# Attention and mixture layer in one kernel: two buffers for reloaded rows, a fuller start on TensorE, and a later last product

## The chip, the cores and the metric

The kernel runs on one core of a Trainium2 chip. The metric is the time of one execution on the device, in microseconds (us); lower is better. A core has five engines that work side by side, each through its own list of instructions in order: TensorE (PE, matrix products, with PEld for its weight loads), VectorE (DVE), ScalarE (ACT), GpSimd (POOL) and SyncE (SP). Transfers (DMA) are issued by SP, ACT and POOL. An instruction that waits holds up all that stands behind it in its engine's list. This is also so for a transfer that waits: it holds up the transfers behind it in the same issuing list.

## The reference

The input is x, 1024 rows of 512 numbers in float32, and the kernel computes

```
xn = layernorm(x)
q, k, v = xn @ w_q, xn @ w_k, xn @ w_v      # 32 query heads, 8 key/value heads, 128 wide
attn = softmax(causal(q k^T / sqrt(128))) v   # 4 query heads share one key/value head
x = x + layernorm(attn @ w_o)
h = layernorm(x)
w = weights of 8 experts from the 8 largest of 15 router probabilities of h
y = h @ base_W^T + base_b + 2 * sum over experts of w_e * (h A_e^T) B_e^T
out = x + layernorm(y)
```

## The kernel before, in words

The 1024 rows are eight tiles of 128. At the start all rows of x are loaded and normalized in place (`input_norms`, L238), and each tile is turned by four TensorE transposes and one copy by ACT into `xnT` (`input_turn`, L262). Values come from `project_v`, keys from `project_k`, and queries for two row tiles at once from `project_q` (two banks, each holding two of the four heads of a key/value head).

The attention is then worked off in 64 blocks. A block is one key/value head g and one row tile t, with its four query heads (`blocks`, L88). The list runs over heads 0 to 5 with all eight tiles each; the last sixteen blocks, 48 to 63, alternate between heads 6 and 7 in pairs of tiles: (6,0) (6,1) (7,0) (7,1) (6,6) (6,7) (7,6) (7,7) (6,4) (6,5) (7,4) (7,5) (6,2) (6,3) (7,2) (7,3). The width of a block's tiles is 128 (t+1), so a block can be told in the profile by its widths.

Each block has four parts n (`scores`, L358): 32 rows of all four heads. A part is a product q k^T on TensorE (`s`), a mask addition and a maximum on VectorE (L378, L380), an exponential on ACT (L385), a reciprocal on POOL (L387), and, one part later, the scaling by ACT (L391) and a 32 by 32 transpose on VectorE into the tile `T` (L394). After the fourth part `to_keys` (L403) issues 16 transfers that put T into the layout `K`; they are issued by SP, and for the very last block by SP and ACT in turn (L399). Two blocks later `weighted_values` multiplies K with v (`po`). T and K have one buffer for even and one for odd tiles.

Work between the parts of a block is laid down in the loop of L698: the list `then` is cut by its estimated cost into four shares, one behind each part (`run_share`). It holds projections for coming blocks, the product with v of block i-2, and the output projection of earlier blocks, which for heads 0 to 6 is done for a pair of row tiles (`project_o_pair`, seven products in place of eight), and for head 7 by `project_o`.

When head 7 is done for a row tile, its attention output is complete, and the second half of the layer begins for this tile: `reload_x` (L533) brings the row of x back at i = k+2 for block k, issued by SP at the beginning of block i, ahead of the K transfers of block i-1; `project_o` at k+3 is followed by `ffn_norms`, which adds x at L519; `ffn_router` comes at k+5, `ffn_out` at k+6 or k+7, and `ffn_store` (L593), again issued by SP at the beginning of a block, at k+7 or k+8. `ffn_out` consists of two products with base_W, a transpose of the expert rows (`ptw`, copied by ACT into `hwT`), two more products, and a last product with hwT, after which VectorE computes y, its norm and the sum into `acc` (L586 to L588). The last four of the eight row tiles are completed behind the loop, from L727 on.

The order of instructions on VectorE, ACT and POOL that is not fixed by the program (marked by `keep`) is set by a scheduler when the kernel is built; transfers and TensorE's instructions stay in the program's order.

Of the kernel before, what the change touches and what calls it, by code (L numbers as in the profile page):

```python
# [22 lines left out]
def kernel(  # L23
# [74 lines left out]
    def transpose(*args):  # L98
        keep(nc.tensor.transpose(*args))

    def load(dst, src, by=nc.sync):
        keep(by.dma_start(dst, src))  # L102
# [86 lines left out]

    def prepare_mask():  # L190

        mask = const.tile([P, P], F32, tag="mask", name="mask")
        make_causal_mask(nc, mask, mask_val=MASKED)
        for h in range(R):
            keep(nc.vector.tensor_copy(smask[ts(h, SQ), :], mask[ts(h, SQ), ts(h, SQ)]))
# [29 lines left out]
    def bank(name):  # L225
        return ps_m.tile([P, 512], F32, tag="pm", name=name)
# [35 lines left out]
    def input_turn(t):  # L262
        transposed(xnT[t // TPB][:, :, ts(t % TPB, P)], x_in[:, t, :], f"x{t}")
# [18 lines left out]
    def project_v(gv, t):  # L282
        def finish(pm):
            v = vs[gv, t] = act.tile([P, GV * D], F32, tag="v", name=f"v_{gv}_{t}", bufs=NT + 2)
            nc.scalar.copy(v, pm)

        def term(c):
            return xnT[t // TPB][:, c, ts(t % TPB, P)], weights["v", gv, c]

        return chained(  # L290
            lambda: bank(f"pv_{gv}_{t}")[:, : GV * D],
            [lambda c=c: term(c) for c in range(KC)],
            finish,
            GV * D,
        )

    def project_k(g, qb):
        def finish(pm):
            kT = kTs[g, qb] = act.tile([P, QB], F32, tag="kT", name=f"kT_{g}_{qb}", bufs=2 * NQB)
            nc.scalar.copy(kT, pm)  # L300

        def term(c):
            return weights["k", g][:, c, :], xnT[qb][:, c, :]

        return chained(
            lambda: bank(f"pk_{g}_{qb}"), [lambda c=c: term(c) for c in range(KC)], finish
        )

    def project_q(g, u):

        pm = {}

        def get(j):
            if j % 2 == 0:
                pm[0] = bank(f"pq_{g}_{u}_{j}")
            return pm[0][:, ts(j % 2, PQ)]

        def finish(j):
            if j == 0:
                qTs[g, u] = act.tile([P, PQ // SQ, R, SQ], F32, tag="qT", name=f"qT_{g}_{u}")  # L320
            if j % 2:
                nc.scalar.mul(  # L322
                    qTs[g, u][:, :, j - 1 : j + 1, :].rearrange("p s h q -> p h s q"),
                    pm[0].rearrange("p (h s q) -> p h s q", h=2, q=SQ),
                    scale,
                )

        def term(j, c):
            w = weights["q", j // 2]
            assert w[0] == g  # L330
            rhs = xnT[u * PQ // QB][:, c, ts(u % (QB // PQ), PQ)]
            return w[1][:, c, ts(j % 2, D)], rhs

        work = []
        for j in range(R):
            terms = [lambda j=j, c=c: term(j, c) for c in range(KC)]
            if j == 0:
                ends = lambda pm: finish(0)
            else:
                ends = lambda pm, j=j: finish(j)  # L340
            work += chained(lambda j=j: get(j), terms, ends, PQ)
        return work
# [15 lines left out]
    def scores(g, t, j):  # L358

        n = t * P + (j + 1) * SQ  # L360
        full = (t + 1) * P
        name = f"{g}_{t}_{j}"

        if t < TPB and j % 2:
            s = score_tile.pop(0)[:, QB:]
        else:
            s = ps_s.tile([P, S], F32, tag="s", name=f"s_{name}")
            score_tile[0] = s
        for c0 in range(0, n, QB):
            w = min(QB, n - c0)  # L370
            matmul(
                s[:, c0 : c0 + w],
                qTs[g, t // 2][:, (t % 2) * NSUB + j, :, :].rearrange("p h q -> p (h q)"),
                kTs[g, c0 // QB][:, :w],
                start=True,
                stop=True,
            )
        nc.vector.tensor_tensor(s[:, n - SQ : n], s[:, n - SQ : n], smask, ALU.add)  # L378
        nmax = small.tile([P, 1], F32, tag="nmax", name=f"nmax_{name}")
        nc.vector.tensor_reduce(nmax, s[:, :n], AX.X, ALU.max, negate=True)  # L380
        p = act.tile([P, S], F32, tag="p", name=f"p_{name}", bufs=3)
        if n < full:
            nc.gpsimd.memset(p[:, n:full], 0.0)  # L383
        total = small.tile([P, 1], F32, tag="total", name=f"total_{name}")
        nc.scalar.activation(p[:, :n], s[:, :n], AF.Exp, bias=nmax, accum_out=total)  # L385
        rec = small.tile([P, 1], F32, tag="rec", name=f"rec_{name}")
        nc.gpsimd.tensor_tensor(rec, total, neg_one, ALU.pow)  # L387
        finish_scores()

        def finish():  # L390
            keep(nc.scalar.mul(p[:, :n], p[:, :n], rec))  # L391
            if j == 0:
                turned[g, t] = turn_view(turn_tile("T", g, t), t)
            nc.vector.transpose(  # L394
                turned[g, t][:, :, j, :, :].rearrange("p b k q -> p k b q"),
                p[:, :full].rearrange("p (k b q) -> p k b q", b=R, q=SQ),
            )
            if j == NSUB - 1:
                to_keys(g, t, by=two if (g, t) == blocks[-1] else two[:1])  # L399

        score_tile["finish"] = finish

    def to_keys(g, t, by=(nc.sync,)):  # L403

        src = turned.pop((g, t))
        dst = keyed[g, t] = turn_view(turn_tile("K", g, t), t)
        for h in range(R):
            for b in range(NSUB):
                load(dst[ts(b, SQ), h, :, :, :], src[ts(h, SQ), b, :, :, :], by[b % len(by)])

    attnT = {}

# [97 lines left out]
    state = {}  # L510

    def reload_x(t):
        xt = state["x", t] = ffn.tile([P, H], F32, tag="x", name=f"xr_{t}", bufs=1)
        load(xt, x[ts(t, P), :])

    def ffn_norms(t):
# [77 lines left out]
        load(out[ts(t, P), :], acc[t])  # L594


    def projections(i):


        g, t = blocks[i]  # L600
        q, other = [], []
        m = i // 2 + 1
        if i % 2 and m < len(pairs):
            q = project_q(*pairs[m])
        if i < N2:
            if t == 2:
                other += project_k(g, 1)
            if t == 6:
                other += project_k(g + 1, 0)
            if g == 0 and t < 2:  # L610
                other += [(P * KC, lambda n=n: input_turn(n)) for n in range(TPB + 2 * t, TPB + 2 * t + 2)]
                other += project_v(0, 2 + t)
            elif g % GV == 0 and (g or t >= TPB):
                other += project_v(g // GV, t)
        else:
            n = i - N2
            for k, what in ((0, (G - 1, 0)), (2, (G - 2, 1)), (3, (G - 1, 1))):
                if n == k:
                    other += project_k(*what)
            for t in {0: (0,), 1: (1,), 2: (2, 3), 3: (4, 5), 4: (6, 7)}.get(n, ()):  # L620
                other += project_v(g // GV, t)
        return q, other
# [25 lines left out]
    def run(pieces):  # L648
        for _, f in pieces:
            f()  # L650
# [23 lines left out]
    input_norms(range(TPB))  # L674
    prepare_mask()
    input_norms(range(TPB, NT))
    for t in range(TPB):
        input_turn(t)
        if t < 2:
            run(project_v(0, t))  # L680
    run(project_k(0, 0))
    run(project_q(0, 0))
    load_o(0, nc.sync)
    combine_o(0)

# [12 lines left out]
    for i in range(N):  # L698
        loads(i)
        for t in complete(i, 2):  # L700
            reload_x(t)
        for t in complete(i, 7, 8):
            ffn_store(t)
        q, other = projections(i)
        pv = attend(i - 2) if i >= 2 else []
        o, o_pair, ends, begins = [], [], [], []
        for t in complete(i, 3):
            o = project_o(*blocks[i - 3])
        if i % 2 == 0 and i >= 4 and blocks[i - 4][0] < G - 1:
            o_pair = project_o_pair(*pairs[i // 2 - 2])  # L710
        for t in complete(i, 6, 7):
            ends = sum(ffn_out(t), [])
        for t in complete(i, 5):
            begins = ffn_router(t)

        then = begins[:1] + q + ends + o + weave(o_pair, begins[1:] + other + pv)
        for n in range(NSUB):
            scores(*blocks[i], n)
            run_share(then, n, NSUB)
        if i == NT:  # L720
            prepare_ffn()

        if i >= NT and blocks[i - 2][1] == 0 and blocks[i - 2][0] < G - 1:
            combine_o(blocks[i - 2][0])
# [63 lines left out]
```

## Time and profile before

| | us |
|---|---|
| median of three runs | 1124.17 |
| lowest, highest | 1122.99, 1276.79 |
| the profiled execution | 1121.25 |
| its span in the profile | 1119.5 |
| TensorE busy | 1073.8 |
| VectorE busy | 639.3 |
| ACT busy | 464.3 |
| POOL busy | 230.2 |

The profile is of one execution. Its lines name the engine, the line of the program, the operation and the tiles (result <- operands), then the count, busy time, and in brackets how long the engine was idle before and what ended that. A row of the stretches gives the stretch, its length, then for PE, PEld, DVE, ACT and POOL the busy time and the number of instructions, the clock granted to TensorE (1.00 is full), the busy share of the transfer engines, and GB/s. A row of waits gives who waited for whom: the total, the number of times and the longest. A row of the timeline gives the start, the length from the first to the last instruction of the group, and the group. SPq is SP's list of transfers, as far as it is issued.

A float32 product shows as two matmul instructions, a transpose as one.

### The profile page before, as it was taken

The numbers are of one execution on the slowest core, as the hardware profiler recorded it, in microseconds if no ns is written. First come the engines' busy times: TensorE is split into PE (matmuls) and PEld (weight loads), VectorE is DVE, ScalarE is ACT, GpSimd is POOL, SyncE is SP. The second block draws the span as 40 slices with busy tenths as digits, with TensorE's granted clock in tenths as the row PEclk, the third lists the DMA queues.
The fourth block names the chain that finished last, engine by engine and source line by source line (L and its number), as shares of the span: only waits on it lengthen the run. The fifth ranks groups of instructions, "written<-read, shape, count | busy, mean of one in ns | idle before, by whom it ended". The sixth has DMA issues, their size and how long they took to land.

```text
span 1119.5 us, 12689 instructions
## 1 busy us (share of the span) xinstructions
PE 1073.8 (96%) x3816; PEld 702.7 (63%) x3816; DVE 639.3 (57%) x1285; ACT 464.3 (41%) x985; POOL 230.2 (21%) x524
## 2 busy tenths in 40 slices
PE   6999999999999999999999999999999699999796
PEld 4676666667676666666676666666776356466353
DVE  4466545664566545665465546665346556766665
ACT  2544434444354434444344434543335343353310
POOL 5311113111321113111221113111131111211200
PEclk9999999999999999999999999999999899999998
DMA  6145332555135332555135332556241743552420
GB/s 208 34 109 131 76 86 56 146 127 109 34 97 136 79 85 57 125 139 116 36 88 137 87 85 57 133 137 155 62 121 50 173 116 73 146 137 53 99 75 29
DMA packets 79380, 111.82 MB, mean 100 GB/s; under 512 B 18176, under 2 KB 50960, under 8 KB 79312
## 3 DMA queue, kind: packets, MB, share of 16 engines
q1 hardware_dynamic: 53552, 82.38, 31.8%
q10 hardware_dynamic: 25424, 27.79, 8.1%
q0 software_dynamic: 336, 0.83, 0.2%
q8 instruction: 31, 0.51, 0.2%
q14 instruction: 37, 0.30, 0.1%
HBM read 33.34 MB, written 2.10 MB: 32 GB/s over the span
## 4 chain that ended last, share of the span: by engine, by line
PE 84%; DVE 5%; ACT 4%; SPq 3%; POOL 1%; issue 1%; DMA 1%; ACTq 0%; POOLq 0%; DVEq 0%
PE po L96 20%; PE s L96 18%; PE pq L96 17%; PE pv L96 5%; PE pk L96 5%; PE pa L96 4%; PE pe L96 4%; SPq L102 3%; PE pc L96 2%; PE pb L96 2%; PE pd L96 2%; PE pf L96 2%; ACT p L385 2%; PE pO L96 2%; DVE nmax L380 1%; DVE T L394 1%
## 5 line engine op out<-in xcount | busy, mean ns | idle before, releaser
L385 ACT ACTIVATE p<-s,nmax 128x32 f32<-128x32 f32 (+31 forms) x256 | 179.6, 702 | 440.3 <-DVE nmax L380 401.8
L394 DVE STREAM_TRANSPOSE T<-p 128x128 f32<-128x128 f32 (+7 forms) x256 | 198.5, 776 | 218.8 <-ACT p L391 193.1
L96 PE MATMUL po<-K,v 128*128 128x512 f32 x576 | 279.2, 599 | 15.9 <-DMA K<-T 14.8
L96 PE MATMUL s<-kT,qT 128*128 128x512 f32 (+15 forms) x768 | 274.2, 466 | 6.0 <-ACT p L385 5.3
L387 POOL TENSOR_TENSOR rec<-total,neg_one 128x1 f32<-128x1 f32 x256 | 143.7, 562 | 637.2 <-ACT p L385 636.9
L96 PE MATMUL pq<-xnT,wq 128*128 128x256 f32 x1024 | 234.9, 379 | 0.0
L96 PEld LDWEIGHTS s<-kT,qT 128*128 128x128 f32 x768 | 145.5, 191 | 134.1 <-issue 110.3
L96 PEld LDWEIGHTS pq<-xnT,wq 128*128 128x128 f32 x1024 | 193.1, 190 | 38.7 <-issue 15.6
L391 ACT ACTIVATE p<-p,rec 128x32 f32<-128x32 f32 (+31 forms) x256 | 185.6, 725 | 2.9 <-POOL rec L387 2.7
L380 DVE TENSOR_REDUCE nmax<-s 128x1 f32<-128x32 f32 (+31 forms) x256 | 180.7, 706 | 7.4
L96 PEld LDWEIGHTS po<-K,v 128*128 128x128 f32 x576 | 107.9, 191 | 91.7 <-issue 75.5
L378 DVE TENSOR_TENSOR s<-s,smask 128x32 f32<-128x32 f32 x256 | 49.1, 192 | 148.8 <-PE s L96 148.3
L96 PE MATMUL pv<-wv,xnT 128*128 128x256 f32 x256 | 69.8, 388 | 1.3 <-ACT xnT L236 1.3
L322 ACT ACTIVATE qT<-pq 128x512 f32<-128x512 f32 x64 | 38.0, 593 | 66.4 <-PE pq L96 66.3
L96 PE MATMUL pk<-xnT,wk 128*128 128x512 f32 x128 | 64.6, 594 | 0.7 <-ACT xnT L236 0.7
L383 POOL MEMSET p<- 128x96 f32 (+2 forms) x192 | 29.0, 152 | 166.5 <-DVE T L394 160.5
L96 PE MATMUL pa<-wo,attnT 128*128 128x256 f32 x224 | 61.9, 385 | 0.0
L419 ACT COPY attnT<-po 128x512 f32<-128x512 f32 x64 | 37.2, 581 | 54.1 <-PE po L96 47.4
L96 PEld LDWEIGHTS pv<-wv,xnT 128*128 128x128 f32 x256 | 48.9, 194 | 11.9 <-issue 2.7
L96 PEld LDWEIGHTS pa<-wo,attnT 128*128 128x128 f32 x224 | 41.0, 190 | 17.8 <-issue 13.9
L385 ACT ACTIVATION_READ_ACCUMULATOR p<-s,nmax 128x1 f32 x256 | 49.7, 194 | 0.0
L96 PE MATMUL pe<-wo,sums 128*128 128x256 f32 x112 | 32.2, 379 | 0.0
(101 smaller groups left out, 731.5 us busy)
## 6 DMA issues: line engine op xcount, KB each, us to landing
K<-T SPq DMA_DIRECT2D x128, 128.0 KB, 2.4
K<-T SPq DMA_DIRECT2D x128, 112.0 KB, 2.3
wq<-in_w_q_dram ACTq DMA_DIRECT2D x27, 512.0 KB, 4.8
K<-T SPq DMA_DIRECT2D x128, 96.0 KB, 2.2
K<-T SPq DMA_DIRECT2D x128, 80.0 KB, 2.1
K<-T SPq DMA_DIRECT2D x120, 64.0 KB, 2.0
wo<-in_w_o_dram ACTq DMA_DIRECT2D x28, 256.0 KB, 3.8
K<-T SPq DMA_DIRECT2D x128, 48.0 KB, 1.9
```

The source lines that it names most:

```text
L96: keep(nc.tensor.matmul(*args, **kw))
L102: keep(by.dma_start(dst, src))
L322: nc.scalar.mul(qTs[g, u][:, :, j - 1 : j + 1, :].rearrange("p s h q -> p h s q"), pm[0].rearrange("p (h s q) -> p h s q", h=2, q=SQ), scale,)
L378: nc.vector.tensor_tensor(s[:, n - SQ : n], s[:, n - SQ : n], smask, ALU.add)
L380: nc.vector.tensor_reduce(nmax, s[:, :n], AX.X, ALU.max, negate=True)
L383: nc.gpsimd.memset(p[:, n:full], 0.0)
L385: nc.scalar.activation(p[:, :n], s[:, :n], AF.Exp, bias=nmax, accum_out=total)
L387: nc.gpsimd.tensor_tensor(rec, total, neg_one, ALU.pow)
L391: keep(nc.scalar.mul(p[:, :n], p[:, :n], rec))
L394: nc.vector.transpose(turned[g, t][:, :, j, :, :].rearrange("p b k q -> p k b q"), p[:, :full].rearrange("p (k b q) -> p k b q", b=R, q=SQ),)
L419: nc.scalar.copy(o, po)
```

## The change

It has six parts.

- `reload_x` takes two buffers (the pool's default) in place of one. The room for it comes from `prepare_mask`, whose mask is now a slice of one of the three softmax tiles `p`.
- At the start, 20 transposes of the identity matrix into a bank that nobody reads stand ahead of the first turn of x.
- The first projections are reordered: tile 2 is turned ahead of the values of tile 1, the queries of the first two heads stand ahead of the keys, and tiles 4 and 5 are turned ahead of the first scores. Tiles 6 and 7 follow in blocks 0 and 1.
- The queries of the second pair of row tiles, all in block 1 before, are divided between blocks 0 and 1.
- The last product of `ffn_out` inside the loop stands four pieces of the other work further on.
- The K transfers of the last block are issued by SP (11) and POOL (5) in place of SP (8) and ACT (8).

```diff
-        mask = const.tile([P, P], F32, tag="mask", name="mask")
+        mask = act.tile([P, S], F32, tag="p", name="mask", bufs=3)[:, :P]
...
-                to_keys(g, t, by=two if (g, t) == blocks[-1] else two[:1])
+                three = (nc.sync, nc.sync, nc.gpsimd)
+                to_keys(g, t, by=three if (g, t) == blocks[-1] else three[:1])
...
-                load(dst[ts(b, SQ), h, :, :, :], src[ts(h, SQ), b, :, :, :], by[b % len(by)])
+                load(dst[ts(b, SQ), h], src[ts(h, SQ), b], by[(h * NSUB + b) % len(by)])
...
-        xt = state["x", t] = ffn.tile([P, H], F32, tag="x", name=f"xr_{t}", bufs=1)
+        xt = state["x", t] = ffn.tile([P, H], F32, tag="x", name=f"xr_{t}")
         load(xt, x[ts(t, P), :])
...
+    later = {}
+
     def projections(i):
...
         m = i // 2 + 1
-        if i % 2 and m < len(pairs):
+        if i == 0:
+            later["q"] = project_q(*pairs[m])
+            q = later["q"][: 2 * KC]
+        elif i == 1:
+            q = later["q"][2 * KC :]
+        elif i % 2 and m < len(pairs):
             q = project_q(*pairs[m])
...
             if g == 0 and t < 2:
-                other += [(P * KC, lambda n=n: input_turn(n)) for n in range(TPB + 2 * t, TPB + 2 * t + 2)]
+                other += [(P * KC, lambda n=TPB + 2 + t: input_turn(n))]
                 other += project_v(0, 2 + t)
...
     input_norms(range(TPB))
     prepare_mask()
     input_norms(range(TPB, NT))
-    for t in range(TPB):
+
+    idle = bank("idle")
+    for n in range(20):
+        transpose(idle[:, ts(n % KC, P)], ident, ident)
+    input_turn(0)
+    run(project_v(0, 0))
+    for t in range(1, 3):
         input_turn(t)
-        if t < 2:
-            run(project_v(0, t))
-    run(project_k(0, 0))
-    run(project_q(0, 0))
+    run(project_v(0, 1))
+    input_turn(3)
+    first_q = project_q(0, 0)
+    run(first_q[: 2 * KC] + project_k(0, 0) + first_q[2 * KC :])
+    for t in range(TPB, TPB + 2):
+        input_turn(t)
     load_o(0, nc.sync)
     combine_o(0)
...
-        then = begins[:1] + q + ends + o + weave(o_pair, begins[1:] + other + pv)
+        rest = o + weave(o_pair, begins[1:] + other + pv)
+        then = begins[:1] + q + ends[:-1] + rest[:4] + ends[-1:] + rest[4:]
```

## The prediction

> **What bounds the kernel now.** I read the page's share of engines, then TensorE's busy time in stretches. A block is one KV head and one row tile; I number the 64 blocks in their order, so "p52" is the softmax of block 52, "T52" its transposed copy, "K52" the 16 transfers that bring T52 into the layout for the product with v.
>
> ```profile
> PE 1073.8 (96%) x3816; PEld 702.7 (63%) x3816; DVE 639.3 (57%) x1285; ACT 464.3 (41%) x985; POOL 230.2 (21%) x524
> ```
> ```profile
> 60.00:460.00 400.00, 397.99 (x1444) 267.77 (x1443) 229.61 (x433) 178.85 (x375) 82.70 (x191) 1.00 0.40 96
> 460.00:860.00 400.00, 399.41 (x1452) 270.37 (x1451) 218.49 (x403) 175.12 (x369) 80.39 (x183) 1.00 0.42 102
> 860.00:960.00 100.00, 87.65 (x277) 50.26 (x276) 61.90 (x119) 38.60 (x69) 15.35 (x37) 0.95 0.46 109
> 960.00:1060.00 100.00, 93.49 (x304) 53.74 (x303) 65.74 (x159) 39.10 (x90) 21.55 (x49) 0.98 0.46 115
> ```
> The first number after the length is TensorE's busy time: 2.6 us of 800 are idle from 60 to 860, so only TensorE's work counts there and the change leaves it alone. The idle time is at the start, in 860 to 1060 (12.35 + 6.51 us, with the clock down to 0.95), and at the end. The waits of TensorE from 860 on, and SP's queue in the same stretch, say why:
>
> ```profile
> PE po L96 <- DMA K<-T: 14.0, 3, 9.3
> PE pf L96 <- ACT hwT L581: 3.2, 3, 2.1
> ```
> ```profile
> SPq L102 <- DVE acc L519: 30.9, 2, 19.6
> ```
> Reloads of x (xr) stand in SP's queue ahead of K transfers. With one buffer, a reload waits until the previous row has been added at L519. The timeline shows the largest case:
>
> ```profile
> 868.14 0.65 DVE L519 TENSOR_TENSOR acc<-acc,xr 128x512 f32<-128x512 f32 x1
> 868.82 0.33 SPq L102 DMA_DIRECT2D xr<-in_x_dram  x1
> 869.26 20.21 SPq L102 DMA_DIRECT2D K<-T  x32
> ...
> 879.67 0.55 DVE L223 TENSOR_SCALAR h<-acc,mv_h,rstd_h 128x512 f32<-128x512 f32 x1 [0.66 <-POOL rstd_h L222]
> 881.27 2.04 PE L96 MATMUL po<-K,v 128*128 128x512 f32 x2 [9.29 <-DMA K<-T]
> ```
> T52 was finished at 853.5 (its last transposes start at 852.42 and take 1.11), but K52 could leave only at 869.26. TensorE stood 9.29 us and was then slow.
>
> [...] eight matmuls of pv took 3.58 us at 8.43 and 1.99 at 13.12; two of po took 2.04 at 881.27 where 0.86 is usual. [...] Here a K transfer costs SP some 0.59 us. [...]
>
> **The change, part by part** (positions are those of the unchanged trace).
>
> Start. The ACT table load ends at 7.68, so the first xnT copy stays at 7.79 whatever the transposes on the identity do. If they warm the array, pv saves 3.58 - 1.99 = 1.6 us; if not, nothing. Either way the next wait is another: rows 4 and 5 are now turned before the first scores.
>
> ```profile
> 23.94 1.34 POOL L454 TENSOR_TENSOR wot<-wo,wot 128x512 f32<-128x512 f32 x1
> 25.24 1.17 POOL L250 TENSOR_TENSOR rstd_x<-ve_x,neg_half 128x1 f32<-128x1 f32 x2
> ```
> ```profile
> 25.83 0.55 DVE L254 TENSOR_SCALAR K_x<-K_x,mv_x,rstd_x 128x512 f32<-128x512 f32 x1 [0.67 <-POOL rstd_x L250]
> ```
> Row 5 is normalized at 26.38, behind the wo subtractions on Pool, which wait for wo until 19.5; the built order of Pool keeps that. Queries before keys fill TensorE to about 24.0 when warm (25.6 cold), then it waits; first scores at 26.9 instead of 28.01: 1.1 us. Two turns (0.43 us each) are then behind it, and half of the next queries stands between the first scores, whose waits on exp were 0.95 and 0.43. Bounds: 0 (these waits stay) and 3.3 us; I take **1.5**.
>
> Reloads, first case. With two buffers the reload of block 51 passes at about 848, K52 leaves at 853.5 and lands 16 x 0.6 + 2.4 us later, near 866; po52 starts at 871.98 without waiting. What is late next is VectorE: from 872 to 880.22 it does the norms of two rows, then a transpose (1.11), mask and maximum (1.3), exp (1.0), so scores of block 55 start at 883.9 where TensorE could at 881 and where they started at 892.40: 8.5 gained. The 2.9 us stand may cool the array; up to 1.2 us are lost. From there I follow both engines to block 56 (906 against 914.14) and find no further wait. Bounds: 4.4 (what VectorE itself gains) and 9.3 + 2.4 of slow clock; I take **7.4**.
>
> Reloads of blocks 55 and 59: no TensorE wait hung on the former. The latter frees K60 (T60 is ready near 1019, K60 left at 1033.66) and K61, which now leaves when T61 is ready, 1038.2, and lands near 1050.6. The waits of 0.92 and 3.79 us before po60 and po61 go, and with the second some 2 us of slow clock (four matmuls in 3.68 us, usual 1.72). But see below.
>
> Last FFN product further on. TensorE waited 2.09 and 0.66 us for hwT; other products now fill this. Bounds 0.5 and 2.9; I take **2.3**. Its price is that y, its norm and the addition to acc (L586 to L588, 3.8 us before: 1039.51 to 1043.27) are later on VectorE, and the store of that row stands in SP's queue ahead of the next block's K transfers. For blocks 50, 51 and 54 the built order puts the addition ahead of the last transpose that K needs: nothing lost. For block 55 it puts it after T62's: K62 no longer waits for VectorE in its own name, but stands behind out55.
>
> ```profile
> 1054.68 0.53 SPq L102 DMA_DIRECT2D out_dram<-acc  x1
> 1055.32 13.69 SPq L102 DMA_DIRECT2D K<-T  x18
> ```
> ```profile
> 1067.04 1.10 PE L96 MATMUL po<-K,v 128*128 128x512 f32 x2 [0.97 <-ACT p L391]
> ```
> Before, K62 left at 1055.32 and set po62 at 1067.04 (the wait is named p, but is K62: 16 x 0.59 + 2.2 after 1055.32 is 1067). In the new order I place VectorE's instructions with the durations above: T62 ends at 52.7 (1052.7), then statistics 0.69, logits 0.17, aggregate 0.18, mask 0.18, three small ones, maximum 0.62, y 0.55, addition 0.69: acc55 at 56.2, K62 from 56.9, landing at 1068.5, 1.5 later than now. TensorE, without the waits of po60 and po61, is there at 1059.2 and stands 9.3 us; as at 881, 2.4 us of slow clock follow. So the waits taken away return at one place: **-3.9** (bounds +6.7 if K62 were not late, -8).
>
> Final K transfers: ACT's eight issues (1067.82 to 1073.44) go; its next work, attnT, needed po62 at 1073.3 anyway. SP issues 11 and Pool 5, done by about 1075, needed at 1084; the cover is 9 us, and Pool has no work until y's rstd. [...] The mask's tile in a softmax buffer costs one memset behind copies that end at 12.9. Both **0**.
>
> Sum: 1.5 + 7.4 + 2.3 - 3.9 = 7.3. The profiled execution took 1121.25 us, so 1114; the median of the runs is 2.9 above it, so 1117. I say **1116**.
>
> **Rivals.** (B) The store does not hold K62: it leaves at 52.7, lands at 1064.9; TensorE still stands 5 us and cools. 3.6 us better: 1112. For it: acc55's operations are short. (C) All waits go and none returns: 3.3 + 9.3 + 2.9 + 0.92 + 3.79 + 1.96, about 22: 1101. Against it: VectorE's full stretch at 872. (D) The time of K52 comes back on VectorE (4.4 only), the start gives nothing: 1121. (E) Slower: the same store. Every us by which acc55 is later than 1056.2 delays K62, and TensorE, by one. Gains outside the end are 11.2, so the change loses when K62 lands over 8.8 us after 1067, acc55 being then at about 1064; at 1069 it would give 1129. Against it: nothing on VectorE that long stands there.
>
> **Chances.** Forecast 0.55, B 0.15, C 0.12, D 0.10, E 0.08. The range leaves out C and E: 1106 to 1123. 2% is about what a measurement of this kernel can tell from no change, 22 us; only the better half of C reaches it (0.06), and a long E on the other side (0.03).
>
> **What would show it.** po52 without a wait at its place, a stand of about 3 us before the scores of block 55, no wait for hwT; SP's store of block 55 waiting for acc, K62 after it, and one wait of about 9 us before po62. The first scores near 27, behind a wait of the turn for row 5. Wrong if po62 shows no wait, if the store waits for much longer, or if the start, with the array warm or not, moves by more than 3 us.

## The result and the profile after

The changed kernel takes 1116.66 us (median of 6 runs, 1116.20 to 1117.02); the kernel before, run beside it, 1122.88. The ratio is 0.9947, 95% interval 0.9933 to 0.9961: some 6 us faster. The profiled execution took 1116.86 us, its span is 1114.9 (before: 1121.25 and 1119.5). So 4.4 us of the gain (4.6 of span) can be read in the two traces. One of the six runs of the kernel before, 1276.79 us, is far from the others and is not in the ratio.

The share of engines on the page, then the stretches (columns as before):

```profile
PE 1079.1 (97%) x3836; PEld 708.3 (64%) x3836; DVE 637.7 (57%) x1285; ACT 464.0 (42%) x985; POOL 231.9 (21%) x529
```
```profile
28.00:60.00 32.00, 29.95 (x119) 21.80 (x119) 14.52 (x42) 16.89 (x51) 9.76 (x24) 0.95 0.13 33
60.00:460.00 400.00, 396.70 (x1438) 266.63 (x1437) 229.08 (x433) 178.68 (x375) 82.41 (x190) 1.00 0.40 95
460.00:860.00 400.00, 399.39 (x1456) 271.01 (x1456) 218.97 (x406) 174.60 (x369) 80.39 (x184) 1.00 0.43 106
860.00:960.00 100.00, 93.97 (x295) 53.63 (x294) 64.85 (x123) 41.80 (x74) 16.42 (x40) 0.98 0.51 120
960.00:1060.00 100.00, 92.91 (x305) 53.94 (x303) 67.39 (x166) 40.35 (x92) 21.83 (x50) 0.98 0.41 100
```

TensorE's idle time in 860 to 960 fell from 12.35 to 6.03 us; 960 to 1060 did not improve, and 28 to 60 now has a clock of 0.95. Below, the array (TensorE) is called slow or cold where the trace grants it a clock of 0.50, and warm at 1.00. Ahead of a trace's first clock record (at 11.69 us in that of the kernel before) it is called so by its times: there the eight matmuls of the first values took 3.58 us, and the next eight 1.99. The waits, first TensorE's and then SP's (who waited for whom: us in total, times, longest):

```profile
PE po L96 <- DMA K<-T: 3.9, 1, 3.9
...
PE pa L96 <- ACT hT L236: 2.8, 1, 2.8
...
PE pf L96 <- ACT hwT L582: 0.4, 1, 0.4
```
```profile
SPq L102 <- DVE acc L589: 23.5, 3, 11.5
```

The wait for K fell from 14.0 to 3.9 us. hwT is down from 3.2 to 0.4, but a wait of 2.8 us for hT is new. SP no longer waits for L519 (now L520), but for L589: stores that wait for their row.

To find where time goes I use one mark, the start of each maximum on VectorE (L380). The lead is how much earlier it starts than in the kernel before; "(54,1)" is the second part of block 54. The last columns are the first matmuls of po62 and the end of the span.

| lead in us | (4,0) | (54,1) | (56,0) | (62,1) | (63,0) | po62 | end |
|---|---|---|---|---|---|---|---|
| changed kernel | -2.2 | -1.6 | 6.6 | 5.7 | 7.2 | 6.4 | 4.6 |
| E1, two buffers alone | -0.4 | 0.0 | 7.4 | 8.3 | 8.5 | 11.5 | 11.3 |
| E4, store behind K | -1.2 | -0.6 | 7.6 | 8.8 | 10.3 | 12.9 | 12.3 |
| E9, best | 1.9 | 2.0 | 10.2 | 9.8 | 11.3 | 13.9 | 13.3 |

The first row says it: the start loses 1.6, K52 brings 8.2, the stretch with the moved product 0.5, and the end gives 2.6 back. The cut at (63,0) favours the moved product: where it is moved, VectorE does y, its norm and acc of block 55 (acc at 1047.81) only behind this mark, in the old order ahead of it. At (62,1) the lead of the changed kernel is 0.9 less than at (56,0).

K52 is as forecast. Timeline of the changed kernel:

```profile
849.36 0.58 SPq L102 DMA_DIRECT2D xr<-in_x_dram  x1
...
855.18 30.00 SPq L102 DMA_DIRECT2D K<-T  x29
...
873.39 1.02 PE L96 MATMUL po<-K,v 128*128 128x512 f32 x2
...
884.81 1.82 PE L96 MATMUL s<-kT,qT 128*128 128x512 f32 x4 [2.29 <-ACT p L385]
```

The reload passes at 849.36, K52 leaves when T52 is done, po52 has no wait, and the scores of block 55 stand 2.29 us for VectorE and ACT.

The start, in the timeline:

```profile
26.30 0.55 DVE L254 TENSOR_SCALAR K_x<-K_x,mv_x,rstd_x 128x512 f32<-128x512 f32 x1 [0.67 <-POOL rstd_x L250]
...
26.99 0.63 PE L99 MATMUL ptx_x<-ident,K_x 128*128 128x128 f32 x4 [1.59 <-DVE K_x L254]
...
28.74 0.55 DVE L254 TENSOR_SCALAR K_x<-K_x,mv_x,rstd_x 128x512 f32<-128x512 f32 x1 [0.44 <-POOL rstd_x L250]
29.20 0.19 DVE L378 TENSOR_TENSOR s<-s,smask 128x32 f32<-128x32 f32 x1
...
38.75 27.76 SPq L102 DMA_DIRECT2D K<-T  x43
...
60.96 0.71 DVE L394 STREAM_TRANSPOSE T<-p 128x512 f32<-128x512 f32 x1 [3.76 <-DMA K<-T]
```

and of the kernel before:

```profile
28.28 0.55 DVE L254 TENSOR_SCALAR K_x<-K_x,mv_x,rstd_x 128x512 f32<-128x512 f32 x1 [0.44 <-POOL rstd_x L250]
28.74 0.20 DVE L378 TENSOR_TENSOR s<-s,smask 128x32 f32<-128x32 f32 x1
...
35.71 26.71 SPq L102 DMA_DIRECT2D K<-T  x40
...
58.78 0.71 DVE L394 STREAM_TRANSPOSE T<-p 128x512 f32<-128x512 f32 x1 [1.85 <-ACT qT L322]
```

The first scores are ready at 27.9, but their mask stands on VectorE behind row 7's normalization and runs at 29.20 (before 28.74, behind the same). K0 leaves SP at 38.75 (before 35.71). Of these 3.0 us, 0.5 lie ahead of the first maximum; 2.6 lie in block 0, which took 9.3 us from there to K0's leaving and 6.7 before. The first transpose of block 3, which needs the T that K1 is still read from, waits until 60.96 (before 58.78).

Before, the view names ACT's copy of qT as what ended that wait, but the transpose doesn't read qT. Its own p was scaled by 58.27, and K1's last transfer landed at 58.60; in the changed kernel these are 58.55 and 60.78. So K1 came last in the kernel before too, if only by 0.3 us, and in both traces the transpose began 0.18 us behind K1's landing.

The end, in the timeline:

```profile
1045.01 0.57 DVE L394 STREAM_TRANSPOSE T<-p 128x384 f32<-128x384 f32 x1
...
1047.81 0.69 DVE L589 TENSOR_TENSOR acc<-y,acc 128x512 f32<-128x512 f32 x1
...
1048.53 0.35 SPq L102 DMA_DIRECT2D out_dram<-acc  x1
...
1048.97 12.68 SPq L102 DMA_DIRECT2D K<-T  x20
...
1060.61 1.10 PE L96 MATMUL po<-K,v 128*128 128x512 f32 x2 [3.91 <-DMA K<-T]
```

T62 is done at 1045.58. K62 stands behind the store, which waits for acc until 1048.5; it landed at 1060.42.

### The profile page after: what moved, and what is told of

It reads as the page before. It is cut to its first block, busy times and chain, and to the rows that moved or that the text cites. A ratio compares the mean times of both kernels' runs of the same rounds, so it can differ in the third digit from the quotient of the medians.

```text
span 1114.9 us, 12741 instructions
## 1 busy us (share of the span) xinstructions
PE 1079.1 (97%) x3836; PEld 708.3 (64%) x3836; DVE 637.7 (57%) x1285; ACT 464.0 (42%) x985; POOL 231.9 (21%) x529
## 4 chain that ended last, share of the span: by engine, by line
PE 81%; DVE 7%; SPq 3%; POOL 3%; ACT 3%; DMA 2%; issue 1%; ACTq 0%; POOLq 0%; DVEq 0%
PE po L96 19%; PE s L96 18%; PE pq L96 16%; PE pv L96 5%; PE pk L96 4%; PE pa L96 4%; PE pe L96 4%; SPq L102 3%; PE pb L96 2%; PE pc L96 2%; PE pd L96 2%; PE pO L96 2%; DVE T L394 2%; PE pf L96 2%; ACT p L385 1%; POOL wot L455 1%
## 5 line engine op out<-in xcount | busy, mean ns | idle before, releaser
L380 DVE TENSOR_REDUCE nmax<-s 128x1 f32<-128x32 f32 (+31 forms) x256 | 180.7, 706 | 7.3
```

## The experiments

Times are medians, 4 to 6 runs each; each ratio is to the kernel before, measured beside it (1121.8 to 1122.9).

| | kernel | us | ratio | interval |
|---|---|---|---|---|
| | changed kernel | 1116.66 | 0.9947 | 0.9933 to 0.9961 |
| E1 | two buffers alone | 1111.34 | 0.9911 | 0.9897 to 0.9926 |
| E2 | changed, old start | 1116.24 | 0.9949 | 0.9937 to 0.9962 |
| E3 | changed, product in old place | 1114.86 | 0.9936 | 0.9919 to 0.9953 |
| E4 | changed, store behind K | 1111.61 | 0.9906 | 0.9893 to 0.9919 |
| E5 | changed, second queries in block 1 | 1116.13 | 0.9950 | 0.9934 to 0.9966 |
| E6 | changed, no products on the identity | 1116.32 | 0.9949 | 0.9935 to 0.9963 |
| E7 | changed, wo subtractions later | 1114.98 | 0.9939 | 0.9924 to 0.9955 |
| E8 | E4 + E7, old order of the start | 1108.61 | 0.9888 | 0.9872 to 0.9905 |
| E9 | E4 + E7 + E11 | 1108.55 | 0.9881 | 0.9868 to 0.9893 |
| E10 | two buffers + store behind K | 1114.43 | 0.9926 | 0.9913 to 0.9940 |
| E11 | changed, K0 and K1 by SP and Pool | 1115.59 | 0.9940 | 0.9925 to 0.9956 |
| E12 | two buffers + K63 by SP and Pool | 1113.01 | 0.9920 | 0.9905 to 0.9935 |

**E1. The buffers alone.**

```diff
-        mask = const.tile([P, P], F32, tag="mask", name="mask")
+        mask = act.tile([P, S], F32, tag="p", name="mask", bufs=3)[:, :P]
...
-        xt = state["x", t] = ffn.tile([P, H], F32, tag="x", name=f"xr_{t}", bufs=1)
+        xt = state["x", t] = ffn.tile([P, H], F32, tag="x", name=f"xr_{t}")
```

> The kernel before with the two buffers for reloaded rows (and the mask in a softmax tile) alone. Theory: this part carries more than the whole gain, and the start and the last product give some of it back. In the changed kernel the lead grew by 9.2 us between blocks 54 and 55 (scores of block 55 at 884.81 in place of 892.40, 1.57 us having been lost before). So 1122.9 - 9, with little more from K60 and K61: 1112 to 1115, po52 without a wait. Rival of the record (7.4 at K52, and a wait of 9 us before po62 that swallows the rest of the reloads' gain): 1115 to 1116. Rival that VectorE keeps half: 4.4 only, 1118.5.

1111.34: more than the whole change gains, by about 4 us. Its timeline:

```profile
871.84 1.02 PE L96 MATMUL po<-K,v 128*128 128x512 f32 x2
...
883.26 3.45 PE L96 MATMUL s<-kT,qT 128*128 128x512 f32 x4 [2.29 <-ACT p L385]
...
1044.01 16.64 SPq L102 DMA_DIRECT2D K<-T  x24
...
1055.54 1.10 PE L96 MATMUL po<-K,v 128*128 128x512 f32 x2 [0.87 <-ACT hT L236]
```

The same stand of 2.29 us before the scores of block 55 is followed here by a slow array (3.45 us; 1.82 in the changed kernel), and the lead at (56,0) is still 7.4. At the end the waits before po60 and po61 are gone and K62 leaves as T62 is done (the last line is po62; its wait is named hT, but K62 landed at 1055.34, 0.2 us ahead of it), so the lead grows from 8.5 to 11.3 where the changed kernel's falls from 7.2 to 4.6. The rival on record, that the end swallows the reloads' gain, falls for this kernel: what swallows it comes with another part.

**E2. The old start.** The start's lines, the split of the second queries and the turns are those of the kernel before; the rest is the changed kernel.

> The changed kernel with the start of the kernel before (no products on the identity, old order of turns, keys and queries, second queries all in block 1, turns 4 to 7 in blocks 0 and 1). Theory: the new start loses; the mark of block 3 is 2.18 us later than in the kernel before, 1.57 of it for good. So 1.6 to 2.2 us faster than the changed kernel, 1114.5 to 1115.1. Rival, the step on record (the start gives 1.5): slower than the changed kernel, 1118.

In the trace the start's loss is gone: lead -0.15 at (54,1) in place of -1.57, and 1.2 us of it is left in the span (1113.7). The medians cannot show it (0.9949 and 0.9947). The step on record, +1.5, does fall: it asked for 1118, and the runs lie between 1115.33 and 1116.51. The expected 1.6 to 2.2 is not in the medians. Against E1 this kernel has the moved product and K63's issuers more, and is 4 us slower: the loss is in these.

How much a start loses differs from execution to execution. At (54,1) the changed start was 1.6 us behind in the changed kernel, 3.0 in E3 and 0.6 in E4, which have the same start; the old start was 0.0 to 0.2 behind in E1, E2 and E12 and 2.0 in E10.

**E3. The product in its old place.**

```diff
-        rest = o + weave(o_pair, begins[1:] + other + pv)
-        then = begins[:1] + q + ends[:-1] + rest[:4] + ends[-1:] + rest[4:]
+        then = begins[:1] + q + ends + o + weave(o_pair, begins[1:] + other + pv)
```

> The changed kernel with the last FFN product back in its old place. Theory: moving it exchanged the waits for hwT (2.1 and 0.7 us) for a wait of 2.8 us for hT, and held K62 behind the store of block 55; undone, the hwT waits return, the hT wait and the wait of 3.9 us before po62 go: same or 1 to 3 us faster, 1113.5 to 1116.5. Rival of the record (the product's new place is worth 2.3, and holding K62 costs more at the end): 1111 to 1114 if K62 was the larger, 1119 if the 2.3 was.

1114.86, inside the theory's range, but the interval overlaps the changed kernel's, and runs went from 1110.90 to 1117.65. The traces say more: the hwT wait is back (2.96 us at the longest), the hT wait is gone. K62 leaves as T62 is done (1047.8), but po62 still waited 2.55 us for it and was slow afterwards: in the old place acc stands ahead of T62 on VectorE, and T62 was done 2.2 us later than in the changed kernel (1.4 of it is this execution's later start). That wait I had expected to go.

**E4. The store behind K.** The product stays in its new place.

```diff
-        for t in complete(i, 7, 8):
-            ffn_store(t)
...
             scores(*blocks[i], n)
+            if n == 0:
+                for t in complete(i, 7, 8):
+                    ffn_store(t)
```

> The changed kernel with the store of a finished row issued behind the K transfers of the block before (after the first part's scores) in place of ahead of them. Theory: T62 was done at 1045.58 and K62 left at 1048.97 because the store stood ahead of it and waited for acc; K62 leaves 3.4 us earlier, the wait of 3.9 us before po62 goes and with it some slow clock: 1112 to 1113.5. Rival: something else is late there next (scores of the last part waited 2.8 us for p, and were slow after it): gain below 1 us, 1116 to 1117.

1111.61: 0.4% or 4.6 us faster than the changed kernel, the intervals apart. Its timeline at the end:

```profile
1041.91 0.57 DVE L394 STREAM_TRANSPOSE T<-p 128x384 f32<-128x384 f32 x1
...
1042.54 10.16 SPq L102 DMA_DIRECT2D K<-T  x16
...
1044.71 0.69 DVE L589 TENSOR_TENSOR acc<-y,acc 128x512 f32<-128x512 f32 x1
...
1052.80 0.53 SPq L102 DMA_DIRECT2D out_dram<-acc  x1
...
1054.12 1.10 PE L96 MATMUL po<-K,v 128*128 128x512 f32 x2 [0.52 <-ACT p L391]
```

VectorE's order is the same (T62, then acc), but K62 no longer waits for acc: it leaves 0.1 us after T62 in place of 3.4, po62 waits 0.52 in place of 3.91, and from (63,0) to the end the lead grows by 2.0 where it fell by 2.6. The store's place is shown to be the cost: 4.6 us, by the ratios and by the trace from (63,0) on.

**E5. The second queries in block 1.** `projections` as in the kernel before; turns and order of the new start kept.

> The changed kernel with the second queries all in block 1 again (the rest of the new start kept). Theory: the queries between the parts of block 0 spread its softmax, so that K0 leaves SP at 38.75 in place of 35.71, and SP's row of 40 transfers makes T of block 3 wait for K1 (60.96). Undone, K0 leaves near 36, that wait goes, and the mark of block 4 is less than 0.6 us later than in the kernel before, not 1.2 to 3.6 (the changed start three times): 1.5 to 2 us faster than the changed kernel. Rival: the loss is from the wait for row 5 ahead of the first scores, not from the queries: K0 leaves near 37.5 and the loss stays.

No change (1116.13). K0 left at 37.15, half of the way back, and T of block 3 still waited for K1 until 60.51. The loss at (4,0) was 1.7. These are the rival's numbers, but its reading, that the queries in block 0 are not the cause, is not shown: in this execution the array was slow from 27.2 to 34.0 us after the wait for row 5, which kept the parts of block 0 apart. From the first maximum to K0's leaving, block 0 took 6.6 to 7.0 us in the six executions of the old order, 8.9 to 9.3 in the seven of the new, and 7.9 here, in spite of the slow array. So, as far as one execution tells, half or more of what block 0 lost belongs to the queries in it.

**E6. No products on the identity.**

```diff
-    idle = bank("idle")
-    for n in range(20):
-        transpose(idle[:, ts(n % KC, P)], ident, ident)
```

> The changed kernel without the 20 products on the identity. Theory: they do warm the array (first values in 1.99 in place of 3.58 us), but the first maximum stands on VectorE behind the normalization of row 7, which waits for Pool, 28.97 before and 29.43 after: without them first values take 3.6 us again and the first maximum and the time do not move (within 0.5 us). Rival: the 1.6 us are real, and the kernel is 1.6 us slower, 1118.

As the theory says: the first values take 3.64 us again, the first maximum is at 28.86 (29.43 with them), the time stays (1116.32). The 0.6 us between the maxima are not the array's: Pool's subtractions on wo, which wait for its load, started at 19.38 here and at 19.97 there. What the warm array gains waits for VectorE: without the products there is no wait for row 5 any more.

**E7. The wo subtractions behind block 1**, their order fixed. These are the four subtractions on Pool (L455) that prepare the weights of the output projection.

```diff
     load_o(0, nc.sync)
-    combine_o(0)
...
+        if i == 1:
+            combine_o(0)
...
-            nc.gpsimd.tensor_tensor(dst, p, q, ALU.subtract)
+            keep(nc.gpsimd.tensor_tensor(dst, p, q, ALU.subtract))
```

> The changed kernel with the four subtractions on wo moved on Pool behind block 1. Theory: rows 4 to 7 then don't wait for Pool behind wo (until 19.5); the turn of row 5 doesn't wait, the first maximum is near 26 in place of 29.43, K0 leaves 3 us earlier and T of block 3 doesn't wait for K1: 3 to 4 us faster than the changed kernel, 1113. Rival: the wait returns on Pool (5.2 us of subtractions ahead of the reciprocals of block 2): no more than 1 us.

1114.98, 0.08% less than the changed kernel, inside the noise. In the trace rows 6 and 7 are normalized by 21.3, the first maximum is at 27.08, and block 2 leads by 2.3. Then it is lost at two places: 1.0 us at the end of block 2, where Pool's subtractions (42.4 to 47.7) stand ahead of its reciprocals, and 1.2 at block 3:

```profile
58.72 0.71 DVE L394 STREAM_TRANSPOSE T<-p 128x512 f32<-128x512 f32 x1 [3.07 <-DMA K<-T]
```

So 2.2 us are gained against the changed kernel's start (1.3 against the same start in E4), not 3 to 4, and SP takes the place of Pool.

**E11. K0 and K1 shared by SP and Pool**, the changed kernel otherwise.

```diff
-                to_keys(g, t, by=three if (g, t) == blocks[-1] else three[:1])
+                to_keys(g, t, by=three if (g, t) in (blocks[0], blocks[1], blocks[-1]) else three[:1])
```

> The changed kernel with the K transfers of blocks 0 and 1 shared by SP (11 each) and Pool (5 each), and nothing else. Theory: in all kernels T of block 3 could be written 21.6 to 23.4 us after K0 left SP, which is 32 transfers of SP; with 22 it can be 6 us earlier, so the wait of 3.76 us for K1 goes, and the mark of block 4 is 0.3 later than in the kernel before (as at block 2), not 2.18: 1.5 to 2 us faster than the changed kernel. Rival: the transfers' own landing, not their issue, sets it: no change, 1116.7.

Its timeline:

```profile
37.56 32.86 SPq L102 DMA_DIRECT2D K<-T  x41
...
37.83 2.51 POOL L102 DMA_DIRECT2D K<-T  x5 [0.24 <-DVE s L378]
...
57.38 0.71 DVE L394 STREAM_TRANSPOSE T<-p 128x512 f32<-128x512 f32 x1 [1.38 <-ACT p L391]
```

The wait for K1 is gone and (4,0) leads by 1.2. In the changed kernel, E3, E4, E5, E6 and E7 this transpose began 21.6 to 23.4 us after K0 left, whenever that was; here 19.8, and no longer because of a transfer. SP's issuing, some 0.6 us for each of 32 transfers, is shown to set block 3: from (3,0) to (4,0) the six kernels lost 0.7 to 3.8 us of their lead, and this one gained 0.3. But the time gains 1 us only (1115.59), and the intervals overlap. Of the 3.0 us more at (54,1), 1.2 stood already at (2,0), where these transfers don't yet count; 0.8 were lost by (56,0), as the array was slow this time after the wait before the scores of block 55 (2.75 us for them in place of 1.82), and 1.3 behind po62, which waited for K62 as before (3.73 us) and then took 2.05 us in place of 1.10.

**E10. Two buffers and the store behind K**: E1 with E4's edit.

> The kernel before with two buffers, and the store of a finished row behind the K transfers; the last product in its old place, the old start. Theory: in the old place acc of block 55 is added ahead of T62 on VectorE, so the store holds nothing: same as two buffers alone, 1111.3 (1110.5 to 1112). The last product's new place costs 5 only because of the store. Rival: the store holds K62 there too: 1 to 3 us faster.

1114.43, worse than both expected. In the trace the store indeed holds nothing in either kernel (K62 leaves as T62 is done). What is different is the array. The first two rows of values in E10's timeline, and po62:

```profile
8.25 3.78 PE L96 MATMUL pv<-wv,xnT 128*128 128x256 f32 x8 [0.68 <-ACT xnT L236]
...
13.56 3.78 PE L96 MATMUL pv<-wv,xnT 128*128 128x256 f32 x8 [0.67 <-ACT xnT L236]
...
1058.22 1.93 PE L96 MATMUL po<-K,v 128*128 128x512 f32 x2 [2.44 <-DMA K<-T]
```

The second row took 1.99 us in the kernel before; the start lost 2.0 us to it. The clock was halved again at 915.0, which E1 did not have. Before po62 the array was warm where it was slow in E1, so it waited 2.44 us for K62 in place of 0.87 and was slow after it. From (63,3) to the end this kernel loses 3.5 us of its lead, E1 1.8. So the profiled execution is explained, but that the store is worth nothing there rests on the trace, not on the medians. A cost of the store's late place in the old order is not excluded.

**E12. Two buffers and K63 by SP and Pool.**

> The kernel before with two buffers and the last K transfers by SP (11) and Pool (5) in place of SP and ACT. Theory, as on record: these transfers have 9 us of cover, so nothing against two buffers alone (1111.3, within 1). Rival: Pool's issues or SP's three more transfers reach po63 or y's norm: 1 to 3 us slower.

1113.01, 1.7 above E1; the intervals overlap. From (63,3) to the end E1 loses 1.8 us of its lead and E12 2.1, po62 starts as in E1 plus the 0.2 of the start. So in these traces K63's issuers cost no more than 0.3 us.

**E8 and E9. All that helped.** E8: E4 and E7 with the old order of the first projections and the second queries all in block 1 (the identity products kept). E9: E4, E7 and E11 on the new start.

> Two buffers, last product further on, store behind K, wo later, products on the identity, but the order of turns, keys and queries of the kernel before. Theory: 1111.6 (store behind K, with the new start losing 0.6 to 3) less that loss and less the 1.5 that the warm array gives once Pool doesn't stand in the way: 1107 to 1109. Rival: the start can't give anything, as SP's K transfers set block 3: 1110 to 1111.

> The changed kernel with the store behind K, the wo subtractions behind block 1, and the K transfers of blocks 0 and 1 shared by SP (11 each) and Pool (5 each). Theory: the store is worth 5 (1111.6), wo 2.2 in the marks, and with SP's row shorter block 3 doesn't wait for K1, so that the 2.3 us by which block 2 leads after the wo edit are kept: 1107.5 to 1109. Rival: Pool's transfers stand ahead of its reciprocals and delay the softmax of blocks 1 and 2: 1110 to 1112.

1108.61 and 1108.55. Both medians lie in the range of their theory. E8's profiled execution was its slowest (1112.96), with both rows of values at 3.78 us although the identity products ran, so its trace can't show what the warm array gives. E9 has the lowest ratio of the study, level with E8: 1.2% faster than the kernel before and, by the ratios, 7.4 us faster than the changed one; its four runs lie within 0.5 us. Of its 2 us at (54,1), E11's transfers and E7's subtractions have both their share: at (2,0) it led by 3.9, and the subtractions, now with K1's transfers on Pool, cost 3.1 at the end of block 2, of which 1.0 came back by (4,0). That part of E9's rival is true.

## Why the prediction was right, and where not

The total was right (1116 forecast, 1116.66 measured, range 1106 to 1123), but not by all of its steps. In the traces, 4.6 us were gained against 7.3 in the sum:

| step | forecast | measured |
|---|---|---|
| start | +1.5 (0 to 3.3) | -1.6 |
| K52 | +7.4 (4.4 to 11.7) | +8.2 |
| last product further on | +2.3 (0.5 to 2.9) | +0.5, blocks 56 to (63,0) |
| end | -3.9 (-8 to +6.7) | -2.6, from (63,0) |
| last K transfers, mask | 0 | 0.3 at the most (E12) |

The last row lies within the row above it. The cut at (63,0) between the product and the end is mine: the wait before po60 lies in the third row, forecast in the fourth, and at (62,1) the third row would be -0.9. The two rows together are -2.1 against -1.6. The profiled execution was forecast at 1114 and took 1116.86. What met the median was the 2 us by which the forecast was raised, as the median of the kernel before lay above its profiled execution; the changed kernel's lies 0.2 below. That is luck. And the forecast's "2% is about what a measurement of this kernel can tell" is too coarse: the intervals here are some 0.13% to each side.

**Start: wrong, outside its bounds.** The step asked when TensorE can do the first scores, and found 26.9 (27.45 measured). What failed is the bound of 0, that waits behind it at the most stay. Three things follow the first scores that I had not followed to their end. The mask stands behind the normalizations of rows 6 and 7 on VectorE, which wait for Pool; the list of before showed it (28.28 for row 7, 28.74 for the mask), so an earlier product could gain nothing. The queries that fill TensorE's waits between the first scores also put these scores apart: block 0 took 2.6 us longer. And block 0's end sets when K0 leaves, and K0 sets block 3 through SP's queue; in the unchanged kernel K1 was already the last to come there. E6 shows that the warm array is hidden. E7 and E11 lead at (54,1) by 0.7 and 1.4 us, where three executions of the changed start are 0.6 to 3.0 behind: Pool's subtractions and SP's 32 transfers each hold the start. The term to follow was the issue queue, which I had followed at the end and not at the start.

**K52: right**, with its cause, place and next limit: VectorE, a stand of 2.29 us (forecast 2.9). The 1.2 us that the step set aside for a cooled array (an estimate from po52's 2.04 us behind its stand of 9.29, where 0.86 is usual) were not needed in the changed kernel, and were in E1. The reload of block 59 freed K60 and K61 as forecast.

**Last product: wrong in mechanism.** "Other products now fill this" holds for the wait named hwT, not for the time. Timeline of the changed kernel:

```profile
913.99 0.57 ACT L236 COPY hT<-ptx_h 128x512 f32<-128x512 f32 x1
...
914.45 0.27 ACT L582 COPY hwT<-ptw 128x128 f32<-128x128 f32 x1
914.61 0.92 PE L96 MATMUL pa<-wo,attnT 128*128 128x256 f32 x2 [2.78 <-ACT hT L236]
```

and the kernel before:

```profile
920.62 0.57 ACT L236 COPY hT<-ptx_h 128x512 f32<-128x512 f32 x1
...
921.09 0.27 ACT L581 COPY hwT<-ptw 128x128 f32<-128x128 f32 x1
```

ACT copies hT and hwT one after the other, both behind the exponential and the scaling of a part. The piece that now follows, pa, waits for ACT's copy of hT, although it doesn't read hT: by the program it takes the next of three banks, and the copy empties that bank. So TensorE waits for the same engine at the same place, and gets free less than half a us earlier. I had looked for pieces that don't need hwT, not for where their bank comes from. In the changed kernel the array was slow after this wait, from 914.95 to 918.36. What the move is worth is isolated by no run. E4, with the new place, and E1, with the old, both stayed warm here: from (56,0) to (62,1) they gained 1.2 and 0.9 us, to (63,3) 6.5 and 5.7. So the traces leave 0.3 to 0.8 us for the move, once nothing else is lost to it, where 2.3 was forecast.

**End: right in mechanism, its size off by 1.3 at that cut.** The store waits for acc, acc stands behind T62 on VectorE, K62 behind the store; all of it was on record, with 3.5 us from the end of T62 to that of acc (measured 2.9). TensorE stood 3.9 and not 9.3 us, since it came 7.7 us after K62 had left and not 2.3: the scores of part 3 had waited 2.82 us for exp, and what followed was slow (1.91 us for two matmuls):

```profile
1051.29 1.91 PE L96 MATMUL s<-kT,qT 128*128 128x512 f32 x2 [2.82 <-ACT p L385]
```

What I called rival B, no holding, was priced at 3.6 us better; E4 measured 4.6. The price was too low by the forecast's own figures: K62 would leave 4.2 us earlier and land as much earlier. Rival E needed acc later than it ever was.

What the sum hid: a start 3.1 us worse, a product and an end together 0.5 worse, and K52 0.8 better. The change as made is worth less than its first part alone.

## What to carry to other kernels

Moving a product further on moves every store that hangs on it; if stores share an issue queue with transfers that the next stage needs, issue the store behind them: here a waiting store held K62 back by 3.4 us, and that cost 4.6. Follow a change at the start through the queue of issues until the first buffer that comes round again, not to the first product. When several edits come together, run the one with the clearest cause alone: here two buffers gave more than the whole. And where a wait is put down to an instruction whose result isn't read, look at when the transfers landed.

## What the runs showed of the hardware

Products on the identity do warm the array: in E3, E4, E7 and E11 one of the 20 took up to 0.47 us at first and 0.27 at last, before any other matmul had run. But the gain is not sure. In the changed kernel, E5, E8 and E9 none of the 20 took less than 0.41, and in E8 the first turn behind them was still slow (0.42 to 0.48 us for a matmul). The first values took 1.99 us in the changed kernel, E5, E9 and E11, and 3.6 to 3.8 in E3, E4, E7 and E8, all with the same 20 products.

The same holds after waits: 2.29 us before the scores of block 55 were followed by 1.82 us of matmuls in one kernel and 3.45 in another; after 2.78 us of waiting for hT, scores and pl took 2.23 and 1.70 us in the changed kernel, 1.19 and 1.20 in E4. In the clock records of the kernel before and of the changed kernel every spell between two changes is a whole multiple of 3.41 us, from 1 to 259 of them. I cut the traces into windows of this length, from the first change on. So cut, the wait of 2.29 us lies, but for 0.1 us, in one window in E1 (first two rows) and in two in the changed kernel (last two; the columns are length, TensorE's busy time, clock, transfers):

```profile
879.74:883.15 3.41, 1.22 (x3) 1.00 0.91 202
883.15:886.56 3.41, 3.30 (x5) 0.50 0.71 155
...
880.82:884.23 3.41, 1.70 (x4) 1.00 0.94 207
884.23:887.64 3.41, 2.83 (x12) 1.00 0.97 210
```

TensorE was idle for 2.19 us of E1's window, and the next one had half the clock; it was idle for 1.71 us in the changed kernel's, and the clock stayed. In the traces of the kernel before and the changed kernel together 636 windows ran at full clock. Ten of them were followed by half the clock, each with 1.96 us idle or more; the other 626 had 1.79 us idle or less. Of the ten windows at half clock that another followed, eight had no idle time, and full clock came behind them; two had 2.6 and 3.4 us idle, and half the clock stayed. So in these two traces some 2.0 us of idle time within a window were enough.

What looks like chance is thus, as far as these traces tell, where the windows fall. By estimate, a window at half clock costs at most 1.7 us, half of 3.41; E1's scores of block 55 lost 1.63 (3.45 in place of 1.82). This is a likely reason, though not shown, why runs of E1, E3 and E12 spread over 5 to 7 us, and why edits of 1 to 2 us could be told in the traces only.

What waited held up what stood behind it in its list. In the changed kernel TensorE had done the third scores of block 3 by 59.27, but VectorE's mask for them ran at 61.59, behind the transpose that had waited 3.76 us for K1. And K62, whose T62 was done at 1045.58, left SP at 1048.97, behind the store that waited for acc.
